# Chunks of 64 keys for the decay product of a state-space mixer: quarters of the matmul array, and 20 pieces of decay table

## The chip, the cores and the metric

The kernel runs on one core of a Trainium2 chip. The time is the device time of one execution in microseconds, and the median of three runs is compared. Besides the runs there is one profiled execution with a trace of every instruction.

The engines named here are TensorE (matmuls, PE in the views; PEld is its weight load), VectorE (DVE), ScalarE (ACT), GpSimd (POOL) and SyncE (SP), which issues all DMA transfers of this kernel. Each engine takes its instructions in the order in which they stand in its queue.

## The reference

Three layers follow each other on x, four batches of 256 positions by 512 features: a causal attention with an adapter, a state-space mixer, and a clustered feed-forward layer. A feed-forward layer with the same weights also stands between attention and mixer. The change is in the mixer alone. Cut to what matters, the mixer computes for each of its 128 heads (64 features each, 8 groups of heads that share B and C):

```python
dt  = softplus(dt + dt_bias);  dA = dt * A            # (batch, position, head)
cum = cumsum(dA)                                      # in chunks; only differences are used
scores[i, j] = (C[i] . B[j]) * exp(cum[i] - cum[j]) * dt[j]     for j <= i, else 0
y[i] = sum_j scores[i, j] * x[j]  +  D * x[i]
```

The reference carries a state from chunk to chunk; written out over the 256 positions of a batch this is one masked product of keys j and queries i. B, C and x are projections of the normalised input with a short causal convolution of four taps and a SiLU; y is gated by the SiLU of another projection, normalised by group and projected back to 512 features. Everything is float32.

## The kernel before, in words

**Tiling.** The 8192 features of the mixer are 64 blocks of 128, two heads a block. The main loop (`for i in range(NB + 1)`) takes one block a step. All four batches, 1024 positions, stand side by side on the free axis, so a tile is 128 by 1024. Eight steps make a group, and for each group one block of B and one of C is projected in addition.

**Projections.** `projected` makes a 128 by 1024 tile `pp` in PSUM (two buffers). A product of full precision is three fp32r matmuls of 512 columns per 128 features of the input (`mm3`, L113 to L115), so one projection is 24 matmuls. The weights are fetched as `wr`, split into a high and a low part by `split` (L105 a cast on ACT, L106 a subtraction on DVE, in the first steps on POOL), and held in three buffers `w`.

**Convolution.** `conv` scales `pp` on ACT (L962), adds three taps on DVE (L969) and applies the SiLU on ACT in place (L973). The result of x is the tile `acc`, tag `x2`.

**Scores of a group.** `scores` (L983 to L988) multiplies B and C per batch and keeps three blocks of 128 keys by 128 queries: first keys with first queries, first keys with second queries, second keys with second queries. A triangle of ones (`tri`) zeroes what lies above the diagonal. The table `gm` has 4 x 3 x 128 = 1536 columns.

**Decay of a head.** The cumulative sum `cum` of all heads is written to DRAM (`cumd`); `rows` reads the row of a head back, repeated on all 128 partitions (`r`, 512 KB, two buffers). `differences` makes the table `em` of 1536 columns: on DVE four subtractions for the last block (L1001), on POOL one affine select that masks the first (L1005), on ACT eight exponentials of 128 columns with a bias per key (L1010, L1013) and one of 512 columns (L1011). `weighted` multiplies `em` by `gm` on DVE (L1017). Three buffers hold `em`, so a table can be begun when the product has read an older one.

**Turn and product.** `turned` transposes x on TensorE (`trx`, L1028) and multiplies it by dt on DVE (`xd`, L1029). `product` (L1043) is 16 float32 matmuls: per batch and block of 128 keys one for each of the two heads, whose 64 features are 64 columns of the array. The trace shows two records for each. `gated` adds D times x (L1053), multiplies by the gate's SiLU `gt` (L1163 makes it, L1056 uses it), sends the result to DRAM (`spill`) and sums its squares (ACT L1065, POOL L1066).

**Back projection.** For the group before, `recall` fetches pieces `gr` from DRAM, `split` makes `gh` of them, and `partial` multiplies (`pog`, 24 matmuls for 128 positions); `scaled` adds the result to `x` (L1114). Most steps hold one such part.

**Order.** The source gives the dependences and a rough order; a scheduler orders the instructions of each engine, and the queues are then fixed. Tables of ACT's functions are loaded (`ACT_TABLE_LOAD`) wherever an exponential follows a SiLU in ACT's queue or the reverse.

**Setup.** Ahead of the loop the kernel makes dt and the cumulative sum per head, transposes them (L941, L950, L954) and keeps them by key in `col_t` and `dt_t`.

## Time and profile before

| What | Value |
|---|---|
| Runs | 1879.57, 1879.75, 1885.73 us; median 1879.75 us |
| The profiled execution | 1881.0 us, span 1879.2 us, mean granted clock 0.989 |
| Attention and first feed-forward layer | about 0 to 330 us |
| Mixer's setup and first projections | about 330 to 420 us |
| Mixer's loop | about 420 to 1790 us |
| Last layer | the rest |
| Product `pyy`, L1043 | 189.1 us busy, 2048 records |
| Weighting, L1017 | 228.6 us busy, 128 instructions of 1786 ns |
| Exponentials of 128 columns, L1010 and L1013 | 165.0 and 166.5 us busy, 512 each |
| Subtractions, L1001 | 137.9 us busy, 512 |

The profiled execution's own time lies 1.25 us above the median of the runs. A group's line in the profile gives line, engine, operation, output and inputs, shape and count, then busy time in us and the mean of one in ns, and then how long its engine stood idle just ahead of it and for whom. The busy time of matmuls is a union of intervals that include the pipeline's latency, so single durations can't be summed.

### The profile page before, as it was taken

How to read it: one execution, taken by the hardware profiler on the slowest of the kernel's cores; microseconds unless marked ns; L12 is line 12 of the kernel's file. 1: busy time of each engine (PE TensorE's matmuls, PEld its weight loads, DVE VectorE, ACT ScalarE, POOL GpSimd, SP SyncE). 2: the span in 40 equal slices, each digit the busy share in tenths (PEclk: the TensorE clock that was granted, in tenths of full speed). 3: DMA queues.
4: the chain of work that ended last, by engine and by line, in shares of the span. 5: the costliest groups of instructions: out<-in, count | busy, mean ns of one | idle time of the engine just before them, and what ended most of it. 6: DMA issues, size and time to landing. Idle time of an engine off the chain costs nothing.

```text
span 1879.2 us, 29896 instructions
## 1 busy us (share of the span) xinstructions
PE 1812.6 (96%) x10706; PEld 1450.4 (77%) x10706; DVE 1464.7 (78%) x2317; ACT 1367.7 (73%) x2809; POOL 397.0 (21%) x380
## 2 busy tenths in 40 slices
PE   7999988899999999999999999999999999999997
PEld 6777767677778787887787787878887888787787
DVE  5566667789997779778977787778778877877777
ACT  6666675378897778777876786778777876877754
POOL 6332230012321111221221121112221211121200
PEclk9999999899999999999999999999999999999999
DMA  4000000135555545544545455544444545455341
GB/s 144 1 1 1 22 15 13 37 99 170 185 182 166 156 148 173 152 157 146 185 140 172 144 173 155 165 147 162 157 157 140 179 145 164 152 159 161 113 125 50
DMA packets 152772, 240.35 MB, mean 128 GB/s; under 512 B 12464, under 2 KB 77616, under 8 KB 152624
## 3 DMA queue, kind: packets, MB, share of 16 engines
q1 hardware_dynamic: 152624, 238.44, 39.8%
q8 instruction: 84, 1.38, 0.3%
q14 instruction: 64, 0.52, 0.1%
HBM read 202.75 MB, written 35.65 MB: 127 GB/s over the span
## 4 chain that ended last, share of the span: by engine, by line
PE 79%; DVE 9%; ACT 7%; issue 2%; DMA 2%; POOL 1%; SPq 0%; DVEq 0%; ACTq 0%; POOLq 0%
PE pp L113 12%; PE pp L114 12%; PE pp L115 12%; PE pyy L1043 9%; PE pog L113 6%; PE pog L115 6%; PE pog L114 6%; PE trx L1028 3%; ACT e L475 2%; DVE acc L969 2%; PE ptr L491 1%; DMA wor<-in_wout_dram 1%; PE pq L113 1%; PE pq L114 1%; PE pq L115 1%
## 5 line engine op out<-in xcount | busy, mean ns | idle before, releaser
L113 PE MATMUL pp<-mx,w 128*128 128x512 f32 (+1 forms) x1160 | 465.2, 401 | 7.9 <-DVE acc L969 7.4
L114 PE MATMUL pp<-mx,w 128*128 128x512 f32 (+1 forms) x1160 | 454.0, 391 | 0.0
L115 PE MATMUL pp<-mx,w 128*128 128x512 f32 (+1 forms) x1160 | 453.7, 391 | 0.0
L969 DVE SCALAR_TENSOR_TENSOR acc<-pp,cw_s,acc 128x1012 f32<-128x1012 f32 (+2 forms) x240 | 305.3, 1272 | 23.0 <-ACT acc L962 22.3
L1017 DVE TENSOR_TENSOR em<-em,gm 128x1536 f32<-128x1536 f32 x128 | 228.6, 1786 | 94.3 <-ACT em L1011 85.9
L113 PEld LDWEIGHTS pp<-mx,w 128*128 128x128 f32 x1160 | 218.4, 188 | 65.7 <-issue 10.2
L1005 POOL TENSOR_SCALAR_AFFINE_SELECT r<-r 128x512 f32<-128x512 f32 x128 | 148.6, 1161 | 521.9 <-DMA r<-cumd 394.8
L1066 POOL TENSOR_TENSOR sq<-sq,acc 128x1024 f32<-128x1024 f32 x55 | 132.6, 2410 | 582.1 <-ACT acc L1065 582.1
L115 PEld LDWEIGHTS pp<-mx,w 128*128 128x128 f32 x1160 | 218.4, 188 | 45.5 <-issue 0.4
L114 PEld LDWEIGHTS pp<-mx,w 128*128 128x128 f32 x1160 | 218.6, 188 | 40.6 <-issue 0.7
L105 ACT CAST w<-wr 128x512 fp32r<-128x512 f32 x144 | 88.5, 615 | 188.9 <-PE pp L114 150.2
L113 PE MATMUL pog<-wo,gh 128*128 128x512 f32 x512 | 204.7, 400 | 0.0
L115 PE MATMUL pog<-wo,gh 128*128 128x512 f32 x512 | 200.0, 391 | 0.0
L1010 ACT ACTIVATE em<-r,col_t 128x128 f32<-128x128 f32 x512 | 165.0, 391 | 48.1 <-PE pyy L1043 46.5
L114 PE MATMUL pog<-wo,gh 128*128 128x512 f32 x512 | 200.0, 391 | 0.0
L1043 PE MATMUL pyy<-em,xd 128*64 128x256 f32 (+1 forms) x2048 | 189.1, 329 | 2.4 <-DVE em L1017 2.4
L1043 PEld LDWEIGHTS pyy<-em,xd 128*64 128x64 f32 x2048 | 133.9, 137 | 63.8 <-issue 21.8
L1013 ACT ACTIVATE em<-r,col_t 128x128 f32<-128x128 f32 x512 | 166.5, 388 | 0.0
L1001 DVE TENSOR_SCALAR em<-r,col_t 128x128 f32<-128x128 f32 x512 | 137.9, 332 | 12.1 <-PE pyy L1043 10.1
L1029 DVE TENSOR_TENSOR xd<-trx,dt_t 128x512 f32<-128x512 f32 x128 | 86.3, 684 | 54.1 <-PE trx L1028 53.9
L106 DVE TENSOR_TENSOR w<-wr,w 128x512 fp32r<-128x512 f32 x139 | 97.6, 703 | 35.9 <-ACT w L105 35.4
L475 ACT ACTIVATE e<-sc,nmx 128x256 f32<-128x256 f32 (+1 forms) x256 | 104.0, 441 | 21.0 <-DVE nmx L469 20.9
(290 smaller groups left out, 3187.2 us busy)
## 6 DMA issues: line engine op xcount, KB each, us to landing
wr<-in_win_dram SPq DMA_DIRECT2D x287, 256.0 KB, 2.8
r<-cumd SPq DMA_DIRECT2D x128, 512.0 KB, 4.1
spill<-gb SPq DMA_DIRECT2D x63, 512.0 KB, 2.8
gr<-spill SPq DMA_DIRECT2D x120, 256.0 KB, 3.5
wor<-in_wout_dram SPq DMA_DIRECT2D x64, 256.0 KB, 3.1
out_dram<-x SPq DMA_DIRECT2D x8, 256.0 KB, 2.3
x<-in_x_dram SPq DMA_DIRECT2D x1, 1536.0 KB, 8.7
gr<-spill SPq DMA_DIRECT2D x8, 192.0 KB, 2.5
```

The lines of the kernel that those rows point to most:

```text
L113: nc.tensor.matmul(o, lh, rh, start=(first and k == 0), stop=False)
L114: nc.tensor.matmul(o, lh, rl, start=False, stop=False)
L115: nc.tensor.matmul(o, ll, rh, start=False, stop=(last and k == n - 1))
L475: nc.scalar.activation(es_[c][:, 2 * j + pr, :], sc[:, j, :], AF.Exp, bias=nm[:, j : j + 1], accum_out=rs[:, c, h : h + 1],)
L969: nc.vector.scalar_tensor_tensor(av[:, :, d:], pv[:, :, : L - d], cw_s[:, ch, tap : tap + 1], av[:, :, d:], ALU.mult, ALU.add,)
L1001: nc.vector.tensor_scalar(e[:, b, 2, :], rv[:, b, 1, :], col_t[:, h, b, 1:2], 0.0, ALU.subtract, ALU.min,)
L1005: nc.gpsimd.affine_select(rv[:, :, 0, :], rv[:, :, 0, :], pattern=[[0, B], [1, P]], compare_op=ALU.is_ge, fill=-1e30, base=0, channel_mult ...
L1010: nc.scalar.activation(e[:, b, 1, :], rv[:, b, 1, :], AF.Exp, bias=col_t[:, h, b, 2:3])
L1013: nc.scalar.activation(e[:, b, 0, :], rv[:, b, 0, :], AF.Exp, bias=col_t[:, h, b, 0:1])
L1017: nc.vector.tensor_tensor(e, e, gm, ALU.mult)
L1043: nc.tensor.matmul(py[d, b, k * P :], xd[:, 2 * b + k, d], es2[hh][:, b, 2 * k : 2 if k == 0 else 3, :].rearrange("p s i -> p (s i)"), sta ...
L1066: (nc.gpsimd if n < NB - 1 else nc.vector).tensor_tensor(sq, sq, x2, ALU.add)
```

## The change

The keys of a batch are now cut into four chunks of 64. Two batches share the 128 partitions: partitions 0 to 63 hold chunks of batch j, partitions 64 to 127 the same chunks of batch 2 + j (u is the half, j is 0 or 1). Per j and chunk c only the queries from the chunk on are kept: 4, 3, 2 and 1 pieces of 64, so ten for each j and 20 pieces of 64 in all, 1280 columns.

- `product` takes 64 keys and 64 features at a time: 32 matmuls of 256, 192, 128 or 64 columns, for two partition halves and two heads, each on its own quarter of the array. The two halves write two PSUM banks.
- `scores` makes `gm` in 20 pieces, without a triangle: 16 matmuls, each half of the keys on its own column half, and eight copies on DVE.
- `differences` makes the 20 pieces: pieces of a chunk with itself (`own`, 512 columns) by one subtraction on DVE, one addition of a mask (`past`) on POOL and one exponential; pieces of the next chunk, where a pair of chunks begins (`next_`, 256 columns), by one subtraction and one exponential; the others by four exponentials of 128 columns, with a bias `end_t`.
- `rows` reads two halves of a row, each repeated on 64 partitions, with four buffers of half the size.
- `conv` of x now keeps `acc` apart (one buffer) and writes the SiLU to `x2` in the new order of positions; `gated` works in two halves of 512.
- The setup writes dt and the cumulative sum in the new order as well; the sum restarts at the same places as before.

```diff
             def scores(bt, ct):
-                gm = p2.tile([P, B, 3, P], F32, name="gm", tag="gm")
...
+                gm = p2.tile([P, 20, Q], F32, name="gm", tag="gm")
+                for j in range(2):
+                    for cs in ((0, 1), (2, 3)):
+                        pg = ps.tile([P, 512], F32, name="pg", tag="m")
...
+                                nc.tensor.matmul(
+                                    pg[u * Q : (u + 1) * Q, at : at + n], bt[:, o : o + Q],
+                                    ct[:, o : o + n], start=True, stop=True,
+                                )
...
             def rows(h):
-                r = p2.tile([P, NT], F32, name="r", tag="r", bufs=2)
-                load(r, cumd[h : h + 1, :].to_broadcast([P, NT]))
+                r = p2.tile([P, 2 * L], F32, name="r", tag="r", bufs=4)
+                for u in range(2):
+                    load(
+                        r[u * Q : (u + 1) * Q, :],
+                        cumd[h : h + 1, u * 2 * L : (u + 1) * 2 * L].to_broadcast([Q, 2 * L]),
+                    )
                 return r
             def differences(h, r):
-                e = p2.tile([P, B, 3, P], F32, name="em", tag="em", bufs=3)
...
+                e = p2.tile([P, 20, Q], F32, name="em", tag="em", bufs=3)
+                own, next_ = pieces_of(e, 0, 4, 4, 7), pieces_of(e, 1, 8, 2, 9)
+                rv = r.rearrange("p (j c i) -> p j c i", j=2, c=4)
+                cv = col_t[:, h, :].rearrange("p (j c) -> p j c", j=2).unsqueeze(3)
+                nc.vector.tensor_tensor(own, rv, cv.to_broadcast([P, 2, 4, Q]), ALU.subtract)
+                nc.gpsimd.tensor_tensor(
+                    own, own, past.unsqueeze(1).unsqueeze(1).to_broadcast([P, 2, 4, Q]), ALU.add
+                )
+                nc.vector.tensor_tensor(
+                    next_, rv[:, :, 1::2, :], cv[:, :, 0::2].to_broadcast([P, 2, 2, Q]), ALU.subtract
+                )
+                for j in range(2):
+                    for c in range(2):
+                        nc.scalar.activation(
+                            piece(e, j, c, 2 - c, 2), rv[:, j, 2:, :], AF.Exp,
+                            bias=end_t[:, h, 2 * j + c : 2 * j + c + 1],
+                        )
+                nc.scalar.activation(next_, next_, AF.Exp)
+                nc.scalar.activation(own, own, AF.Exp)
                 return e
             def product(xd, es2):
-                py = ps_y.tile([P, B, L], F32, name="pyy", tag="pyy")
...
+                py = ps_y.tile([P, 2, 2 * L], F32, name="pyy", tag="pyy")
+                for j in range(2):
+                    for c in range(4):
+                        for u in range(2):
+                            us = slice(u * Q, (u + 1) * Q)
+                            for hh in range(2):
+                                d = slice(hh * PD, (hh + 1) * PD)
+                                nc.tensor.matmul(
+                                    py[d, u, j * L + c * Q : (j + 1) * L].rearrange("p (k i) -> p k i", i=Q),
+                                    xd[us, 4 * j + c, d], piece(es2[hh], j, c)[us],
+                                    start=(c == 0), stop=(c == 3),
+                                )
                 return py
             def gated(n, x2, gt, py, sq):
-                nc.vector.scalar_tensor_tensor(
-                    gb, x2, dh[:, n : n + 1], py.rearrange("p b t -> p (b t)"), ALU.mult, ALU.add
-                )
+                for u, h in enumerate(hs):
+                    k = lambda v: v.rearrange("p (k i) -> p k i", i=Q)
+                    nc.vector.scalar_tensor_tensor(
+                        k(gb[:, h]), pair(x2)[:, :, u], dh[:, n : n + 1], k(py[:, u]), ALU.mult, ALU.add
+                    )
...
-            rr = {h: rows(h) for h in range(2)}
+            rr = {h: rows(h) for h in range(4)}
```

In `conv` of x:

```diff
-                silus.append(nc.scalar.activation(acc, acc, AF.Silu).ins)
-                return acc
+                x2 = p2.tile([P, NT], F32, name="x2", tag="x2", bufs=2)
+                silus.append(nc.scalar.activation(
+                    pair(x2).rearrange("p k u i -> p u k i"),
+                    acc.rearrange("p (u k i) -> p u k i", u=2, i=Q), AF.Silu,
+                ).ins)
+                return x2
```

The new helpers `piece` and `pieces_of` only address pieces of a table: `piece(v, j, c, k, n)` gives n query pieces of chunk c from the k-th on, with a step of 1 or 3 pieces, and `pieces_of` gives every n-th piece for both j at once.

## The prediction

> **What bounds the kernel now.** I read the page's first part, then its chain, then a table by stretches, because 96% busy is an average and matmuls overlap in it. The stretches are four consecutive steps of the mixer's loop over its 64 head pairs, cut where the decay product `pyy` starts.
>
> ```profile
> PE 1812.6 (96%) x10706; PEld 1450.4 (77%) x10706; DVE 1464.7 (78%) x2317; ACT 1367.7 (73%) x2809; POOL 397.0 (21%) x380
> PE 79%; DVE 9%; ACT 7%; issue 2%; DMA 2%; POOL 1%; SPq 0%; DVEq 0%; ACTq 0%; POOLq 0%
> ```
> ```profile
> 950.54:970.83 20.29, 20.29 (x113) 16.22 (x112) 15.98 (x22) 14.82 (x29) 5.73 (x4) 1.00 0.46 143
> 970.83:991.13 20.30, 20.30 (x113) 16.23 (x112) 15.90 (x23) 14.82 (x29) 3.72 (x3) 1.00 0.48 155
> 991.13:1011.42 20.29, 20.29 (x113) 16.22 (x112) 15.55 (x22) 14.81 (x29) 3.77 (x4) 1.00 0.49 155
> ```
>
> The columns are stretch, length, then busy PE, weight loads, DVE, ACT, POOL, then clock and DMA. A regular step is 20.29 us and TensorE has no hole in it; DVE works 15.9, ACT 14.8. Eight such steps make a group, some with fewer or more matmuls. So the mixer (420 to 1790 us) is bound by TensorE, and DVE and ACT have 4.4 and 5.5 us to spare per step. Where that spare time lies is seen in the timeline of ACT: it stands 3.95 us until a projection gives back a weight buffer, and 1.25 us until the product is over.
>
> ```profile
> 1011.31 0.62 ACT L105 CAST w<-wr 128x512 fp32r<-128x512 f32 x1 [3.95 <-PE pp L114]
> 1014.28 1.28 ACT L1010 ACTIVATE em<-r,col_t 128x128 f32<-128x128 f32 x4 [1.25 <-PE pyy L1043]
> 1018.51 1.28 ACT L973 ACT_TABLE_LOAD   x1
> 1019.81 1.06 ACT L973 ACTIVATE acc<-acc 128x1024 f32<-128x1024 f32 x1
> ```
>
> How fast the product runs comes from TensorE's timeline, at a place where its first matmul stands alone (two records[...]) and at one where it is whole:
>
> ```profile
> 922.15 0.65 PE L1043 MATMUL pyy<-em,xd 128*64 128x256 f32 x2
> 922.73 0.50 PE L113 MATMUL pp<-mx,w 128*128 128x512 f32 x1
> ...
> 1011.43 2.82 PE L1043 MATMUL pyy<-em,xd 128*64 128x256 f32 x32
> 1014.18 0.50 PE L113 MATMUL pp<-mx,w 128*128 128x512 f32 x1
> ```
>
> The lone matmul streams 2 x 256 = 512 columns and the next work starts 0.58 us later. The whole product streams, for each head, 4 batches x (256 + 128) x 2 = 3072 columns, and takes 2.75 us. If the two heads, which lie on two column halves of the array, run side by side: (2.75 - 0.58) / (3072 - 512) = 0.85 ns a column and 0.15 us for entering and leaving. One after the other they would need over 5 us, so they do run side by side.
>
> [...] No run here shows quarters of 64 by 64; the nearest row is attention's `sc` (64 rows, two row halves, fp32r), whose eight matmuls take 0.61 us to the next operation, 1536 columns that at the projections' 0.23 us per 512 would need 0.69 us in turn and some edge more. [...] The trace has 1283 ns[...] (load at 1018.51, SiLU at 1019.81), so I use 1.28. [...] The `py` products of attention, 16 matmuls, are over 0.79 us after their start (200.64 to 201.43 us), 50 ns each at most[...]; a burst of 64 no run shows.
>
> **The change part by part.**
>
> *Product.* Per key chunk the queries kept are 256, 192, 128 and 64. A quarter streams 2 batches x 640 x 2 = 2560 columns: 2560 x 0.85 = 2.17, with the edge 2.32 us against 2.75. Gain 0.43 us per step, all on the binding engine: 64 x 0.43 = 27.5 us. It issues 64 matmuls for 32. [...] I take the stream.
>
> *Order of the product.* In the built programs the first product matmul stands alone, parted by projections, at 13 steps; in the trace of before at 11. Two more at 0.58 us: +1.2. In later groups the new `pg` matmuls stand inside a product; some 0.3 us of edges, against 0.43 us that `pg` saves by the same columns: nothing.
>
> *Elementwise work, DVE.* Weighting falls from 1536 to 1280 elements: 128 x (1.67 x 256/1536 = 0.28) = -36 us. Differences: 512 instructions, 138 us, give way to 256 of 512 and of 256 elements, by the rows of 512 at 0.60 and half of it: 128 x 0.93 = 119, -19. Gating in two halves +8. `gm` copies about as before. DVE some 47 us less.
>
> *ACT.* Per head 8 exponentials of 128 (2.59 us) become 4 (1.30) and one of 256, between 0.29 and 0.63, say 0.37; the one of 512 stays. That is -0.92 x 128 = -118 us. But in the built order ACT changes its table 297 times, before 195: a regular step has four loads, not two, since exponentials now stand on both sides of the SiLU of x and of the gate's SiLU. 102 x 1.283 = +131 us. Net +13 us of 1368.
>
> *POOL* trades an affine select (1.16 us) for an add of 512 (`r`, L301: 1.29), which now stands between DVE's difference and ACT's exponential; its own square sum, 2.4 us, is queued there too. By the order both adds are done 5 us before ACT comes to them. *SP* issues two row loads for one, 128 more, with half the bytes (512 to 256 KB a head) and four buffers for two: hidden, rows come two heads earlier. *Setup*: two more ACT copies of 512, +1.
>
> *What is late next.* ACT, DVE and TensorE now hang together in one ring per step, because the queues are in order. Following the built order: three taps 3.90; load 1.28; SiLU of x 1.06; load 1.28; one exponential 0.29; square 1.04; load 1.28; gate SiLU 1.00; load 1.28; exponentials 0.37 and 0.63: 13.4. Then DVE: weighting 1.39, `x` 0.66, `xd` 0.60, two splits 1.20, weighting 1.39, two splits 1.20: 6.4, and the next taps. With 0.15 for handovers this is 20.0 us, and TensorE needs 20.29 - 0.43 = 19.86. So a regular step ends at about 20.0, not 19.86: what waits is the transposition `trx` behind the SiLU. Bounds of the ring: 19.6 if the exponentials of 256 and the weightings come out shorter, 20.7 if [...]a `gh` cast waits for its transfer (it does for up to 4 us nine times before). Some 30 steps are regular: 30 x 0.14 = +4.2. Steps with extra projections have room.
>
> *Sum* against the profiled execution (1881.0 us with a span of 1879.2, 1.25 over the median 1879.75): -27.5 + 1.2 + 4.2 + 1 = -21, so 1860 there, 1859 as a median.
>
> **Rivals.**
>
> *The ring swallows it.* The spare time of ACT goes into table loads, the ring comes to 20.3 to 20.6, and `trx` waits. For it: four loads in a ring that I can close only to a few tenths. Against: none of its durations is a guess by more than 0.1. Regular steps then cost 0 to 0.3 more than before, other steps gain 0.43: 30 x 0.15 - 34 x 0.43 + 2 = -8 in the middle, so 1866 to 1886.
>
> *The quarters do not run four at a time* (ends slower). If the two row halves take turns, a product has 5120 columns: 4.35 + 0.15 = 4.50 us, 64 x 1.75 = +112, some 1990 us. [...] It decides from a product above 2.75 us. For it: no run of float32 on row halves. Against: column halves in float32 and row halves in fp32r overlap[...].
>
> *More comes back than the product.* Fewer DVE passes and earlier rows also end the 9 us in which projections wait behind ACT and DVE: 1842 to 1850.
>
> **How the numbers follow.** First case 0.58, time 1859, own range 1848 to 1869; the ring 0.18; the quarters 0.14; more 0.10. About 0.5% (9.4 us) is what a measurement here can tell from no change. Faster: most of the first case and all of the last, 0.62. Same: part of the ring and the edge of the first, 0.17. Slower: the quarters and the ring's end, 0.21. The range takes the first, the last and the ring, 1842 to 1900, and leaves out the quarters.
>
> **What would show it.** The product: 64 records in about 2.35 us, four starting together; 2.75 or more refutes the main step. Table loads: 297. A regular step between 19.8 and 20.1 us with a small wait of `trx` for the SiLU of x; 20.3 or more with ACT's wait for `pp` gone is the ring. ACT busy near 1380, DVE near 1420.

## The result, and the profile after

The changed kernel takes 1934.76 us (median of four runs, 1932.12 to 1938.86) against 1882.12 us of the kernel before on the same chip: ratio 1.028, 95% interval 1.0251 to 1.0309. It is slower by 2.8%, where the prediction had 1859 us and a range up to 1900. The profiled execution is 1932.1 us with a span of 1930.3.

From the page of the changed kernel, the engines' busy time and the shares of the chain that ended last:

```profile
PE 1816.3 (94%) x12882; PEld 1455.3 (75%) x12882; DVE 1493.3 (77%) x2157; ACT 1396.1 (72%) x2527; POOL 482.0 (25%) x380
PE 46%; DVE 21%; ACT 20%; issue 5%; DMA 4%; POOL 3%; SPq 0%; ACTq 0%; DVEq 0%; POOLq 0%
```

TensorE's part of the chain fell from 79% to 46%: it now waits for others. The product itself does what was forecast. In TensorE's timeline of the changed kernel (start, length, operation, shape, count) a whole product is 64 records, and the next work starts 2.34 us after the product's start (the rounded times of these lines give 2.35), where the kernel before needed 2.75. So the product is 0.41 us shorter:

```profile
1016.92 0.39 PE L115 MATMUL pp<-mx,w 128*128 128x512 f32 x1
1017.23 2.41 PE L1089 MATMUL pyy<-em,xd 64*64 64x256 f32 x64
1019.58 0.50 PE L113 MATMUL pp<-mx,w 128*128 128x512 f32 x1
```

The table by stretches of the changed kernel (stretch, length, busy PE, weight loads, DVE, ACT, POOL, clock, DMA) shows two regular steps, and the step at the end of a group, in which C is projected and the next group's scores are made:

```profile
997.12:1017.23 20.11, 20.05 (x145) 16.13 (x144) 16.31 (x20) 15.79 (x25) 5.79 (x3) 1.00 0.43 131
1017.23:1037.34 20.11, 20.04 (x145) 16.14 (x144) 16.30 (x20) 15.79 (x25) 5.80 (x3) 1.00 0.43 130
...
923.33:949.48 26.15, 21.70 (x157) 16.16 (x156) 22.74 (x30) 17.85 (x27) 5.86 (x3) 0.87 0.42 131
```

A regular step is 20.11 us, as forecast (20.0) and 0.18 less than before. The step at the group's end is cut where the main part of each product starts, since in both kernels the first two records of the second product run ahead. It is 26.15 us; in the kernel before the same step is 19.82 us (stretch 903.80 to 923.62). The seven steps of this kind take 23.1 to 26.7 us, before 18.8 to 20.8. Measured from the end of one product to the end of the next, the span's 51 us split as follows:

| Stretch | before, us | after, us | difference |
|---|---|---|---|
| to the end of the first product | 427.4 | 431.5 | +4.1 |
| first group (nothing yet to project back) | 118.2 | 127.6 | +9.4 |
| groups 2 to 7, each | 179.8 to 180.9 | 185.6 to 187.3 | +35.3 in all |
| last group | 166.3 | 168.7 | +2.4 |
| after the last product | 85.1 | 85.0 | -0.1 |

So there are two questions: why the ends of groups lost 6 us each, and why the product's 0.41 us shows as only 0.2 in regular steps.

Where TensorE's time went is seen when the loop is cut from the end of the first product to the end of the last (stretch, length, busy PE first, then the columns of the table above), in the kernel before and in the changed one:

```profile
427.69:1794.40 1366.71, 1353.63 (x7415) 1080.00 (x7415) 1113.12 (x1514) 1057.04 (x1892) 277.06 (x180) 1.00 0.50 159
```

```profile
431.71:1845.57 1413.86, 1355.77 (x9539) 1083.71 (x9539) 1141.27 (x1352) 1085.90 (x1619) 362.34 (x182) 0.99 0.41 130
```

Length less busy time is what TensorE stands idle: 13.1 us before, 58.1 after. Its busy time has not fallen, although 64 products at 0.41 us less are worth 26 us; part of the reason is a lower clock (0.99 against 1.00 in these lines), as is shown below.

**The end of a group.** The timeline of the changed kernel there (a bracket holds the wait before the instruction and what ended it):

```profile
923.33 2.07 PE L1089 MATMUL pyy<-em,xd 64*64 64x256 f32 x46
...
928.12 2.40 PE L1013 MATMUL pg<-bc 128*64 128x256 f32 x16 [2.71 <-ACT bc L993]
...
930.45 1.54 PE L1089 MATMUL pyy<-em,xd 64*64 64x192 f32 x18
...
933.50 1.70 PE L1013 MATMUL pg<-bc 128*64 128x256 f32 x16
...
934.91 1.02 DVE L1021 COPY gm<-pg 128x256 f32<-128x256 f32 x4 [3.26 <-PE pg L1013]
...
936.51 1.40 DVE L1101 SCALAR_TENSOR_TENSOR gb<-x,dh,pyy 128x512 f32<-128x512 f32 x2
...
937.82 0.68 DVE L1043 TENSOR_TENSOR em<-r,col_t 128x512 f32<-128x512 f32 x1
...
938.65 2.13 POOL L1044 TENSOR_TENSOR em<-em,past 128x512 f32<-128x512 f32 x1 [25.41 <-DVE em L1043]
...
940.82 0.63 ACT L1057 ACTIVATE em<-em 128x512 f32<-128x512 f32 x1 [5.54 <-POOL em L1044]
```

The scores' matmuls `pg` stand in the middle of the product, and TensorE waits there 2.71 us for C's SiLU while the product's last 18 records stand behind. DVE has the copy of the second score tile ahead of everything else and idles 3.26 us for it; the gate `gb` and the subtraction L1043 come after that. POOL's mask add can only follow the subtraction, and ACT stands 5.54 us for POOL, with the square, the gate's SiLU and the other exponentials behind it. The next product is then late: its main part starts at 949.48 us. One wait runs through four queues. Over the loop TensorE waits 17.9 us in seven times for C's SiLU at `pg`, and 12.4 us in seven times for the weighted table ahead of a product.

**A wait can be paid twice.** In stretches after such waits of the same kernel the clock column falls to 0.50 to 0.60:

```profile
928.12:931.20 3.08, 3.08 (x31) 2.42 (x32) 3.04 (x7) 1.91 (x3) 0.00 (x0) 0.50 0.52 180
931.92:934.90 2.98, 2.98 (x16) 1.85 (x17) 0.00 (x0) 2.97 (x9) 0.00 (x0) 0.60 0.17 61
1135.62:1139.63 4.01, 4.00 (x62) 3.72 (x63) 4.01 (x5) 1.91 (x3) 0.00 (x0) 0.57 0.71 215
```

The last of them is a product (62 records) that took 4.0 us instead of 2.3. Between 440 and 1800 us the changed kernel has 16 gaps of TensorE over 1.5 us between starts, 39 us in all; the kernel before has none. Eight of the sixteen were followed by half clock, seven times for 3.4 us and once for 6.8, 31 us together. By an estimate from these lengths, half of their time, that is worth at most 15 us of the 51. In the kernel before the clock doesn't fall in this stretch (1.00). The eight gaps have 2.1 to 3.7 us between starts, but their length alone does not decide: after a gap of 2.13 us at 947 us the next product took 2.3 us, after one of the same length at 1133 us it took 4.0.

### The profile page after: what moved, and what is told of

Read it like the earlier page. It is cut to its first block, busy times and chain, and to the rows that moved or that the text cites. A ratio compares the mean times of both kernels' runs of the same rounds, so it can differ in the third digit from the quotient of the medians.

```text
span 1930.3 us, 33621 instructions
## 1 busy us (share of the span) xinstructions
PE 1816.3 (94%) x12882; PEld 1455.3 (75%) x12882; DVE 1493.3 (77%) x2157; ACT 1396.1 (72%) x2527; POOL 482.0 (25%) x380
## 4 chain that ended last, share of the span: by engine, by line
PE 46%; DVE 21%; ACT 20%; issue 5%; DMA 4%; POOL 3%; SPq 0%; ACTq 0%; DVEq 0%; POOLq 0%
DVE acc L988 8%; PE pp L113 5%; PE pp L114 5%; PE pp L115 5%; PE pog L113 5%; PE pog L115 5%; PE pog L114 4%; ACT L996 2%; ACT x L996 2%; PE trx L1072 2%; PE pyy L1089 2%; ACT e L475 2%; DMA r<-cumd 2%; DVE em L1061 2%; POOL em L1044 2%
## 5 line engine op out<-in xcount | busy, mean ns | idle before, releaser
L1044 POOL TENSOR_TENSOR em<-em,past 128x512 f32<-128x512 f32 x128 | 229.9, 1800 | 1045.7 <-DVE em L1043 992.3
L1061 DVE TENSOR_TENSOR em<-em,gm 128x1280 f32<-128x1280 f32 x128 | 195.8, 1530 | 169.3 <-ACT em L1057 139.6
L988 DVE SCALAR_TENSOR_TENSOR acc<-pp,cw_s,acc 128x1012 f32<-128x1012 f32 (+2 forms) x192 | 244.3, 1272 | 23.3 <-ACT acc L981 20.4
L1052 ACT ACTIVATE em<-r,end_t 128x128 f32<-128x128 f32 x512 | 169.2, 392 | 45.9 <-PE pyy L1089 45.2
L1089 PE MATMUL pyy<-em,xd 64*64 64x192 f32 (+3 forms) x4096 | 176.6, 310 | 13.9 <-DVE em L1061 13.9
L1089 PEld LDWEIGHTS pyy<-em,xd 64*64 64x64 f32 x4096 | 142.9, 138 | 58.5 <-issue 24.1
L1114 POOL TENSOR_TENSOR sq<-sq,x 128x1024 f32<-128x1024 f32 x55 | 137.6, 2501 | 25.2 <-ACT x L1113 25.2
L113 PEld LDWEIGHTS pog<-wo,gh 128*128 128x128 f32 x512 | 96.1, 188 | 24.7 <-ACT rg L1140 2.0
L115 PEld LDWEIGHTS pog<-wo,gh 128*128 128x128 f32 x512 | 96.1, 188 | 20.8 <-DVE gh L106 0.3
L106 DVE TENSOR_TENSOR gh<-gr,gh 128x512 fp32r<-128x512 f32 (+1 forms) x128 | 86.0, 678 | 33.2 <-ACT gh L105 33.2
```

The source lines that it names most:

```text
L113: nc.tensor.matmul(o, lh, rh, start=(first and k == 0), stop=False)
L115: nc.tensor.matmul(o, ll, rh, start=False, stop=(last and k == n - 1))
L988: nc.vector.scalar_tensor_tensor(av[:, :, d:], pv[:, :, : L - d], cw_s[:, ch, tap : tap + 1], av[:, :, d:], ALU.mult, ALU.add,)
L1044: nc.gpsimd.tensor_tensor(own, own, past.unsqueeze(1).unsqueeze(1).to_broadcast([P, 2, 4, Q]), ALU.add)
L1052: nc.scalar.activation(piece(e, j, c, 2 - c, 2), rv[:, j, 2:, :], AF.Exp, bias=end_t[:, h, 2 * j + c : 2 * j + c + 1],)
L1061: nc.vector.tensor_tensor(e, e, gm, ALU.mult)
```

## The experiments

All times are medians, and each ratio is against the kernel before on the same chip. Not all runs were on one chip; the kernel before took 1881 to 1885 us on them, so times that differ by less than some 4 us are not told apart. The three runs with the old product leave out the right pairing of keys: they multiply the new tables in the old pattern and give other values. Gains below are in us between medians; sums by group come from the profiled execution of each run.

| Run | us | ratio to before, 95% interval |
|---|---|---|
| changed kernel | 1934.76 | 1.028 (1.0251 to 1.0309) |
| mask add on DVE | 1914.38 | 1.0168 (1.015 to 1.0186) |
| scores later | 1916.01 | 1.0178 (1.0161 to 1.0195) |
| both | 1904.06 | 1.0099 (1.008 to 1.0118) |
| mask on POOL first | 1907.40 | 1.0116 (1.0092 to 1.014) |
| mask on POOL first, scores later | 1901.54 | 1.0101 (1.0087 to 1.0116) |
| kernel before with a POOL add | 1901.31 | 1.0085 (1.0067 to 1.0103) |
| exponentials together | 1936.55 | 1.0283 (1.0264 to 1.0301) |
| the three | 1916.21 | 1.0164 (1.0144 to 1.0184) |
| exponentials together in the first group | 1904.87 | 1.0114 (1.0096 to 1.0132) |
| exponentials together, pool first, scores later | 1922.11 | 1.0211 (1.0193 to 1.0229) |
| exponentials together, pool first, scores later, SiLU primed | 1917.27 | 1.0182 (1.0158 to 1.0206) |
| changed kernel, old product | 1912.96 | 1.0158 (1.014 to 1.0175) |
| pool first, scores later, old product | 1892.61 | 1.0051 (1.0038 to 1.0065) |
| transposes later | 2035.48 | 1.0813 (1.0788 to 1.0838) |
| pool first, scores later, transposes later | 2021.94 | 1.0743 (1.0724 to 1.0763) |
| pool first, scores later, transposes later, old product | 1893.38 | 1.006 (1.0047 to 1.0073) |
| pool first, scores later, transposes later, exponentials together | 2001.89 | 1.0638 (1.0616 to 1.066) |
| setup's taps later, squares on DVE | 1898.83 | 1.0073 (1.0057 to 1.009) |

### The chain through the mask and the scores

**Mask add on DVE.**

```diff
-                nc.gpsimd.tensor_tensor(
+                nc.vector.tensor_tensor(
                     own, own, past.unsqueeze(1).unsqueeze(1).to_broadcast([P, 2, 4, Q]), ALU.add
```

> The changed kernel with the mask's addition of L1044 on DVE instead of POOL, nothing else. Theory P (the add on POOL stands between DVE's subtraction and ACT's exponential in queues that run in order, and ACT waits 5.5 us for it in the step where a group of eight ends): those steps fall from 26.1 to about 21 us, 7 of them 35 us, so about 1900 us, while the regular step stays at 20.1. Theory G (the scores' matmuls inside the product are what holds that step: PE waits there for C's SiLU, and all else is late after that): the step keeps at least 24 us, and the kernel is at 1920 to 1935. Theory T (ACT's extra table loads set the pace): 291 loads instead of 297, so no more than 5 us, 1930.

Groups 3 to 7 fall from 185.6 to 187.3 us to 182.2 to 185.4, the regular step stays at 20.1, the first two groups together stay where they were (314 us). The gain is 20 us of the 35 that theory P claimed. The steps that it named fall only to 22.2 to 25.2 us and not to 21; the step after each of them is 1 to 2 us shorter in six of seven cases. So P has a part of the cause and not the whole. TensorE still waits for C's SiLU at `pg` (14.5 us in seven times).

**Scores later.**

```diff
-                        gms[g + 1] = scores(bt, ct)
+                        late = (g + 1, bt, ct)
...
                     sqs[m // GB] = gated(m, px2, gt, py, sq)
+                if late:
+                    gms[late[0]] = scores(*late[1:])
+                    late = None
```

> The changed kernel with the scores of the next group written after the product and its gate instead of before them, nothing else. G: PE's wait for C's SiLU inside the product (2.7 to 3.3 us, seven times) goes, and with it DVE's wait for the second scores tile (3.3 us): the step where a group ends falls from 26.1 us to 20 or 21, so about 1895 to 1900 us. P: the add on POOL still follows DVE's subtraction late, so the step stays at 24 us or over and the kernel above 1920. T: 307 loads instead of 297, so no gain, 1935 to 1945.

19 us, and groups 3 to 7 at 182.8 to 183.9. Theory G was right on the place: the step where a group ends falls to 20.0 to 22.2 us. It was wrong on the reason and on the sum, since the step after it grows in six of seven cases, by 0.3 to 3.9 us. TensorE's wait for C's SiLU does not go (16.2 us, against 17.9 in the changed kernel). What goes is its place inside the product. In the timeline of this run the product is whole before the wait, and gate, subtraction and POOL's add come 3.8 to 5.9 us earlier than in the lines shown above:

```profile
922.79 2.41 PE L1089 MATMUL pyy<-em,xd 64*64 64x256 f32 x64
...
927.44 1.52 PE L1013 MATMUL pg<-bc 128*64 128x256 f32 x16 [2.24 <-ACT bc L993]
...
930.61 1.40 DVE L1101 SCALAR_TENSOR_TENSOR gb<-x,dh,pyy 128x512 f32<-128x512 f32 x2
...
933.99 0.68 DVE L1043 TENSOR_TENSOR em<-r,col_t 128x512 f32<-128x512 f32 x1
...
934.82 1.33 POOL L1044 TENSOR_TENSOR em<-em,past 128x512 f32<-128x512 f32 x1 [22.14 <-DVE em L1043]
```

**Both** edits above.

> The changed kernel with both: scores written after the product's gate, mask's addition on DVE. Alone each gave about 20 us (1914 and 1916). If the wait of PE for C's SiLU inside the product (P's and G's chains one after the other) are two separate waits, the gains add: 1896. If both take away the same slack, it stays at 1910 to 1914. The first group is not touched by either (17.3 us a step) and the regular step stays at 20.1.

31 us of the 39 that the two gave singly: mostly two costs, in part the same slack.

**Mask on POOL first.** Same operations and engines, in the other order.

```diff
-                nc.vector.tensor_tensor(own, rv, cv.to_broadcast([P, 2, 4, Q]), ALU.subtract)
                 nc.gpsimd.tensor_tensor(
-                    own, own, past.unsqueeze(1).unsqueeze(1).to_broadcast([P, 2, 4, Q]), ALU.add
+                    own, rv, past.unsqueeze(1).unsqueeze(1).to_broadcast([P, 2, 4, Q]), ALU.add
                 )
+                nc.vector.tensor_tensor(own, own, cv.to_broadcast([P, 2, 4, Q]), ALU.subtract)
```

> The changed kernel with the two operations that make the diagonal pieces swapped: POOL adds the mask to the row of sums first, straight after its load, and DVE subtracts the column afterwards. Same number of instructions, sizes and engines. If the gain of putting the add on DVE came from the order (DVE, then POOL, then ACT in queues that run in order), this gives as much or nearly: 1914 to 1918, with ACT's waits for POOL gone. If it came from POOL's own speed, or from DVE and POOL holding each other up while both run on two operands, no gain: 1930 to 1937.

27 us, more than the order was thought to be worth. ACT's waits for POOL at this exponential are gone (40.4 us in the changed kernel). The groups in this run show a second effect:

```profile
L1043 POOL TENSOR_TENSOR em<-r,past 128x512 f32<-128x512 f32 x128 | 174.1, 1382 | 769.3 <-PE pyy L1089 511.5 <-ACT acc L981 145.1 <-DMA wr<-in_win_dram 84.1
...
L1047 DVE TENSOR_TENSOR em<-r,col_t 128x256 f32<-128x256 f32 x128 | 54.7, 428 | 0.0
```

In the changed kernel the add has a mean of 1800 ns and the subtraction of 256 elements, which DVE takes up while POOL adds, 820 ns. Here they have 1382 and 428. So the order both keeps ACT from waiting for POOL and shortens the add and the subtraction. What each of the two is worth was not separated.

**Mask on POOL first, with scores later.**

> The changed kernel with the mask added on POOL before DVE's subtraction (1907 alone) and the scores written after the gate (1916 alone). The first takes the chain through POOL out of the end of each group (its second step 16.8 us) but leaves PE's wait for C's SiLU inside the product (31 us for the step before it, seven times); the second takes that to 27.3. If the two are separate costs: 1907 - 7 x 3.7 = about 1881. If the slack is shared as with the add on DVE (1904 for the pair): 1898 to 1904. First group unchanged at 17.3 to 17.7 us a step.

6 us less than the mask alone, with intervals that overlap: the slack is shared here. Groups 3 to 7 are at 180.2 to 181.1 us, as in the kernel before (179.8 to 180.6). With that the ends of groups are repaired, and what is left over the kernel before lies ahead of the end of the first product (8.1 us, of which the changed kernel has 4.1), in the first group (+7.8) and in the second (+2.1). The same cut of the loop as above gives:

```profile
435.70:1814.68 1378.98, 1339.77 (x9539) 1075.39 (x9539) 1080.89 (x1350) 1095.60 (x1627) 300.78 (x181) 1.00 0.42 133
```

TensorE stands idle for 39.2 us here, 26 us more than in the kernel before: as much as the shorter products save. It waits 14.8 us for DVE's taps ahead of projections, 12.7 us for C's SiLU at `pg` and 5.6 us for x at the transposes. By an estimate from the clock column (1.00 stands for 0.995 or more, over 1379 us) half clock is worth 7 us at most here, against at most 15 in the changed kernel, so up to 15 of the 33 us gained may be the clock.

**The kernel before with a POOL add.**

```diff
                         ALU.subtract, ALU.min,
                     )
+                nc.gpsimd.tensor_tensor(
+                    e[:, :, 2, :], e[:, :, 2, :],
+                    tri[:, P : 2 * P].unsqueeze(1).to_broadcast([P, B, P]), ALU.mult,
+                )
```

> The kernel before, with one operation added in the same place: after DVE's subtractions for the third block a POOL tensor_tensor of 512 elements (a multiplication by ones, so no value changes) that ACT's exponential of it then waits for. Orders of PE and the 195 table loads stay as they are. If the step through POOL is enough by itself to cost what the changed kernel lost at group ends: plus 15 to 35 us, 1900 to 1920. If POOL's and DVE's contention is what it costs: DVE's busy time rises by 30 us or more. If it needs the late scores ahead of it, the kernel before hides it: 1882 to 1888.

+17 us (23 in the profiled execution, in which this is split). It is not the order at group ends: groups 3 to 7 rise by 0.5 to 1.4 us each, and 11 us fall in the first group. DVE's busy time rises by 115 us although DVE got no work. The groups of this run:

```profile
L1021 DVE TENSOR_TENSOR em<-em,gm 128x1536 f32<-128x1536 f32 x128 | 251.7, 1966 | 94.0 <-ACT em L1015 86.0 <-ACT em L1017 8.0
...
L1005 POOL TENSOR_TENSOR em<-em,tri 128x512 f32<-128x512 f32 x128 | 216.9, 1694 | 445.4 <-PE pp L115 294.3 <-DVE em L1001 133.7 <-ACT acc L1069 17.3
...
L1001 DVE TENSOR_SCALAR em<-r,col_t 128x128 f32<-128x128 f32 x512 | 201.6, 452 | 12.0 <-PE pyy L1047 11.3 <-DMA r<-cumd 0.7
```

The weighting goes from 1786 to 1966 ns and the subtractions from 332 to 452. A POOL step is thus not enough by itself to stop a group's end; in the changed kernel the late subtraction stands ahead of it. But it has a price of its own, paid on DVE.

### Table loads

**Exponentials together.**

```diff
-                    nc.scalar.activation(gt, pp, AF.Silu)
+                    gate = nc.scalar.activation(gt, pp, AF.Silu).ins
...
-                        with tc.issue_after(silus[2]) if i == 0 else ExitStack():
+                        with tc.issue_after(gate):
```

> The changed kernel with the exponentials of a step held behind its gate's SiLU on ACT, nothing else: 167 table loads instead of 297, 130 x 1.28 = 167 us of ACT's busy time less. T: the steps of the first group return from 17.3 to about 15 us (16 us in all), the regular steps from 20.1 to 19.9 (some 40 of them, 8 us), and the end of each group gains the two loads that stand ahead of the weighting (2.6 us, seven times): about 1893 us. G or P: the end of each group stays within 1 us of 26.1, and only the first group gains, so 1910 to 1920. If the loads cost nothing because ACT had room: 1935.

ACT's busy time falls by 180 us to 1215.9 and the time by nothing. The first group gains 3 us (16.8 a step), regular steps 0.1. The second group (6 us more) and what lies outside the groups (6 us more) take it back. The block of twelve exponentials now stands ahead of C's SiLU in ACT's queue, and TensorE's wait at `pg` rises from 17.9 to 32.8 us in seven times, up to 7.1. So the extra table loads are not worth 42 us, as theory T had it. What they cost at the ends of groups is not shown, since the same edit makes TensorE wait longer there.

**The three:** exponentials together, add on DVE, scores later.

> The changed kernel with all three: add on DVE, scores after the gate, exponentials behind the gate's SiLU (167 table loads). In the run with the exponentials together DVE was at 32.4 of 33.6 us in two steps of the first group because its subtraction (0.68 us) took 1.76 us beside POOL's adds. If table loads and POOL's adds together hold the first group, its steps fall from 17.3 to 15.1 to 15.5 (-12 us) and the regular steps to 20.0 or under; with the boundary as in the run of the two alone (1896 expected there) that is 1880 to 1888, about the time of the kernel before. If holding the exponentials back makes the weighting late at the end of a group (36 us for that step when it was done alone), these steps eat the gain: 1900 to 1915.

The second case of the expectation, at its edge: first group 127.2, later groups 180.6 to 184.8, and 12 us slower than without holding the exponentials.

**In the first group only,** with mask on POOL first and scores later: `issue_after(gate)` where `i < GB`.

> As the run before it, with the exponentials held behind the gate's SiLU in the first eight steps only (two table loads a step there instead of four). If the four loads in ACT's ring are what holds the first group at 17.3 us a step, and POOL's adds no longer stand beside DVE's subtractions, five steps fall to 15.1 to 15.6: 9 to 12 us less than the run before it. If DVE (slowed beside POOL) is the next bound there, as with the exponentials together alone (16.8): 2 to 3 us less.

"The run before it" is the one with mask on POOL first and scores later. The result lies within that run's interval. The first group takes 124.7 us instead of 126.0, with steps mostly of 16.7, so the loads were worth some 0.2 us a step there. The timeline of this run holds the clearest view of DVE beside POOL:

```profile
471.66 1.29 DVE L1073 TENSOR_TENSOR xd<-trx,dt_t 128x512 f32<-128x512 f32 x2
...
472.54 2.40 POOL L1114 TENSOR_TENSOR sq<-sq,x 128x1024 f32<-128x1024 f32 x1 [3.08 <-ACT x L1113]
...
472.87 2.62 DVE L1046 TENSOR_TENSOR em<-em,col_t 128x512 f32<-128x512 f32 x1
...
475.41 0.41 DVE L1047 TENSOR_TENSOR em<-r,col_t 128x256 f32<-128x256 f32 x1
```

The subtraction, 0.68 us elsewhere, began 0.33 us after POOL's add and ended 0.55 us after it: it got hardly anywhere until POOL was done. Two of DVE's operations that have one of their two inputs in PSUM did not take longer beside POOL: the two `xd` above took 1.29 us together although the second ran beside the add. In the trace of the changed kernel from 427 to 1800 us `xd` has a mean of 681 ns both in the 73 cases beside a POOL operation and in the 48 others, and in that of the kernel before a tap L969 has 1272 ns both in 22 cases beside one and in 207 others.

### The product's own worth

**Changed kernel with the old product.**

```diff
+                for b in range(B):
+                    for k in range(2):
+                        for hh in range(2):
+                            d = slice(hh * PD, (hh + 1) * PD)
+                            at = (0, 4, 10, 14)[b] + 2 * k
+                            nc.tensor.matmul(
+                                py[d, b // 2, (b % 2) * L + k * P : (b % 2 + 1) * L],
+                                xd[:, 2 * b + k, d],
+                                es2[hh][:, at : at + 4 - 2 * k, :].rearrange("p k i -> p (k i)"),
+                                start=(k == 0), stop=(k == 1),
+                            )
```

> The changed kernel with the product alone put back to the form of the kernel before: sixteen matmuls of 128 keys instead of sixty-four of 64, on the same tables (the values are then not those of the reference: pieces of the two batches are added together). If the product's own gain is real and nothing else hangs on it: 0.43 us more in each of 64 products, 27 us, so 1962 us. If the planner's order hangs on the number of the product's matmuls (with sixteen it puts the scores behind the product again and ACT has 218 table loads instead of 297): the end of each group falls from 26.1 to about 20 us (-42) and the first group's steps to 15.5 (-14), so 1935 + 27 - 56 = 1906 us.

22 us faster, with a product that is 0.41 us slower. (Counted as instructions the two products have 16 and 32 matmuls; the "sixty-four" of the expectation are the new one's records.) It is the expectation's second case: the scheduler's order is another one when the product has sixteen matmuls. It puts `pg` behind the product again (that step, from product end to product end, 27.5 us instead of 31.6 to 33.8).

**Mask on POOL first, scores later, old product.**

> As the first run of this call (mask on POOL first, scores after the gate), with the product alone in the form of the kernel before: sixteen matmuls of 128 keys (the values are then not the reference's). Where PE sets the pace the product's 0.42 us comes back, in 64 products less the five or six of the first group where it doesn't: regular steps 20.3 instead of 20.05, in all plus 15 to 25 us. If the product's gain isn't worth anything in time: within 5 us.

Neither case: 9 us faster than with the new product, the intervals apart. Regular steps rise from 20.05 to 20.3, but the first group falls from 126.0 to 122.0 and the steps after a group's end by 1 to 2 us. The cut of the loop shows what is traded:

```profile
435.71:1806.93 1371.22, 1358.04 (x7530) 1078.79 (x7529) 1091.45 (x1353) 1059.06 (x1598) 322.59 (x181) 1.00 0.42 134
```

TensorE works 18 us more than with the new product and idles 26 us less (13.2 against 39.2). The waits that go are those at `pg` for C's SiLU (12.7 us, here none among the matmuls' waits), and about 5 us each of those for DVE's taps and for x at the transposes. The order of TensorE differs too. Counted from the start of a product in a regular step, the transposes start 9.2 us later with the old product (9.7 in the kernel before). With the new one it is 8.1 us, straight behind the gate's 24 matmuls. The product is 0.41 us shorter, and in the order made for it the four matmuls of the next projection that stood between are gone. The way over ACT and DVE to x has not become shorter. No run has the new product in the order of the old one, so what the order alone costs stays open.

### The transposes

The next runs test theory W: regular steps lose the rest of the product's gain because TensorE waits at the transposes for x, the SiLU's result. In the changed kernel it waits up to 0.5 us there in each of the four regular steps from 997 to 1077 us.

**Transposes later,** on the changed kernel: the first four transposes of a step are written after the output's matmuls.

```diff
                     xd = next(turning)
-                    next(turning)
                 for _ in range(PER.get(gi, 0)):
...
                 if i < NB:
+                    next(turning)
                     for _ in turning:
```

> The changed kernel with the first four transposes of a step written after the output's matmuls instead of before them, nothing else. Theory W: the regular steps fall from 20.1 to 19.87, the sum of PE's own work (35 of them, 8 us), and the step after each group's end by 0.5 to 1 us; the scores' wait and the add on POOL stay: 1915 to 1927. If the transposes' wait only moves to the next thing that needs x (the product's em or the conv's buffers): 1932 to 1937.

**The same on the repaired kernel** (mask on POOL first, scores later).

> Mask on POOL first, scores after the gate (1901.5 together), and the transposes behind the output's matmuls. W: regular steps 19.87 instead of 20.05, the second step of each group 27 instead of 28.3 to 29: 35 x 0.2 + 7 x 1.5 = 17 us less, about 1885. If ACT's ring with its four table loads is the real bound of the regular step, it stays at 20.05 and the kernel above 1898.

100 and 120 us slower, regular steps at 22 to 24 us: a new wait, not a test of the old one. The timeline of the second:

```profile
1019.76 1.49 DVE L1061 TENSOR_TENSOR em<-em,gm 128x1280 f32<-128x1280 f32 x1 [5.39 <-ACT em L1057]
...
1021.17 0.74 DVE L1162 SCALAR_TENSOR_TENSOR x<-pog,rg,x 128x512 f32<-128x512 f32 x1
...
1021.97 0.66 PE L1072 MATMUL trx<-con,x 128*128 128x128 f32 x4 [1.85 <-DVE x L1162]
```

The transposes need the PSUM tile that DVE's L1162 gives back, and L1162 stands in DVE's queue behind a weighting that waits 5.39 us for ACT.

**The same with the old product,** and **with the new one and the exponentials together:**

> The run before it with the product alone in the form of the kernel before (values not the reference's). W: nothing of PE waits in the regular steps of either, so the product's own price shows: 20.28 against 19.87 in some 35 to 42 regular steps and as much in the others that PE sets, 15 to 24 us more than the run before it, about 1903. If the shorter product still isn't worth anything, as in the pair before: 1880 to 1890.

> As e13 with the exponentials of all steps held behind the gate's SiLU (167 table loads instead of 307, 180 us less of ACT's time). If table loads cost no time any more once PE's order has the slack: within 4 us of e13. If ACT's ring still holds steps of the first group and the second of each group: 8 to 15 us less. If holding the exponentials back makes the weighting late at the end of groups (36 us a step when done alone): 5 to 20 us more.

("e13" is the run on the repaired kernel.) The old product's order hardly minds the edit (1893.4), and 194 us less of ACT's work bring only 20 us back. None of the four reads the product's price.

**SiLU primed.** Here TensorE's order stays nearly as it is and x comes early. Both runs hold the exponentials together (mask on POOL first, scores later); the second adds:

```diff
+                with tc.issue_after(first_):
+                    nc.scalar.activation(stat.tile([P, 1], F32, name="prime"), ones[:, 0:1], AF.Silu)
```

where `first_` is the convolution's first operation on ACT.

> Mask on POOL first, scores after the gate, exponentials of all steps held behind the gate's SiLU (167 table loads). Regular steps 20.0 as in the run with the exponentials together, transposes waiting 0.2 us each step. By the runs of the parts: first group 16.8, end of groups 27.4 and 19 to 25, so 1895 to 1910.

> The same with SiLU's table loaded ahead: a one-element SiLU after the convolution's first operation, in each step. The table load leaves the path from DVE's last tap to x, which comes 1.28 us earlier. Theory W: the transposes no longer wait, regular steps fall from 20.0 to 19.87 or less; in all 35 x 0.15 = 5 us, and more where the steps after a group's end hang on x: 5 to 15 us less than the control. If the regular step is held by something else, it stays at 20.0 and the kernel within 3 us of the control.

The control, at 1922 us, missed its own forecast of 1895 to 1910: as in the run of the three, holding all exponentials back costs more than the loads it saves.

The waits of the transposes for x, from the control and then from the primed kernel (total, times, longest):

```profile
PEld trx L1072 <- ACT x L996: 20.1, 43, 0.9
...
PE trx L1072 <- ACT x L996: 4.0, 7, 0.6
```

```profile
PEld trx L1074 <- ACT x L998: 4.5, 8, 0.6
...
PE trx L1074 <- ACT x L998: 1.2, 7, 0.2
```

Regular steps fall from 20.0 to 19.86 us, which is TensorE's own work as it was forecast, 20.29 less 0.43. Theory W holds for regular steps. In the whole time the 5 us between the two lie within the intervals, since other steps moved both ways: in the primed run TensorE waits 23.8 us in six times for DVE's copies of the scores, in the control 0.6 us once.

### Setup and first group

**Setup's taps later, squares on DVE** in the first eight steps, on the run with the first group's exponentials together.

```diff
+                    with tc.issue_after(scan) if inner and ch == 0 else ExitStack():
...
-                    (nc.gpsimd if n < NB - 1 else nc.vector).tensor_tensor(sq, sq, x2, ALU.add)
+                    (nc.gpsimd if GB <= n < NB - 1 else nc.vector).tensor_tensor(sq, sq, x2, ALU.add)
```

> The run with the first group's exponentials held together (mask on POOL first, scores after the gate; 1904.9), with two more edits. In the setup DVE's taps of the first x block are held behind the second half's scan: with batches on the partition halves no transpose of the sums can start before both scans, and the taps stood between them. If that is the setup's loss, the first product ends 3 to 4 us earlier (433.2 before); if not, within 1 us. In the first eight steps the sum of squares is added on DVE instead of POOL: there DVE's subtraction of 0.68 us took 2.62 us while POOL added. If DVE and POOL holding each other up is what keeps these steps at 16.7 us, they fall to 15.3 to 16; if DVE's own work sets them, they stay or rise to 17.5. In all 1893 to 1900 in the first case of both.

The second scan and the first transpose of the sums come 1.3 us earlier than in the run without the two edits, and the first product ends 1.1 us earlier. So the product follows the scan, but the edit moved the scan too little to show whether this is the whole loss. The first group stays at 16.7 us a step although the subtraction is back at 0.68 us, so the squares' add beside DVE is not what holds it. This is the fastest version that has the new product, still 0.73% slower than the kernel before; no run is faster than the kernel before.

## Why the prediction was wrong, step by step

**Product, right in size, wrong in worth.** 0.43 us was forecast, 0.41 measured. The quarters run four at a time, their records starting 6 to 7 ns apart, so that rival falls: in turns the product would have needed 4.50 us by the estimate, and it took 2.34. That the starts of its 64 records would not limit it was the author's estimate; in the product at 1017 us they lie within 2.19 us. The step that failed is "64 x 0.43 = 27.5 us", all on the binding engine. It takes for granted that TensorE stays without holes. Instead its idle time in the loop went from 13.1 to 58.1 us. A regular step gained 0.2 us (29 such steps in groups 2 to 8, 6 us). The rest of a regular step's gain went to the transposes' wait for x. That is shown by the primed pair, with the exponentials held together, where 19.86 us is reached once x comes earlier. In the other 35 steps the gain went into waits at the ends of groups and in the first group. Even with the ends repaired TensorE idles 26 us more than before, which is all that the products save.

**"Inside-product `pg` matmuls: nothing."** The second failed step. I counted columns and edges and not what `pg` waits for, nor what stands behind it: the product's rest, then DVE's gate and subtraction. Moving the scores was worth 19 us. In the built order the place could be seen. The wait for C's SiLU was there before too, 0.64 us at 908 us, but behind the whole product.

**"By the order both adds are done 5 us before ACT comes to them."** The third. In a regular step it holds: in the one from 997 to 1017 us the adds are done 4.9 and 5.6 us ahead. At the end of a group, which I did not check, ACT waited 5.5 us. Putting the add on DVE was worth 20 us, doing it first 27.

**POOL's add at 1.29 us, the subtraction of 256 at 0.33.** Mis-sized: 1.80 and 0.82, since each stands in the other's way; the prediction put that at nothing. Apart from POOL's add the subtraction takes 0.42 us. DVE came out at 1493 us busy instead of about 1420. In the run with the add on DVE, with the add's own 97.7 us taken off, DVE is at 1417. So POOL's add cost DVE 76 us, 51 of them in this subtraction. ACT was 1396 for 1380, with the 297 loads as forecast.

**The ring** of 20.0 us: right for regular steps (20.1). I took the first group as TensorE's own. It is a ring as well there, as the chain of waits through one step of the changed kernel shows (start, length, what; ACT L1211 and ACT L1056 without a tile are table loads):

```profile
479.88 1.26 DVE acc L988
...
484.25 1.27 DVE acc L988
485.52 1.31 DVE gb L1101 x2
486.83 0.61 DVE em L1043
...
487.58 2.49 POOL em L1044
...
490.09 0.63 ACT em L1057
490.73 0.95 ACT x L1113
...
491.69 1.12 ACT L1211
...
492.99 1.02 ACT gt L1211
...
494.03 1.28 ACT L1056
...
495.77 1.13 DVE em L1061
...
497.18 1.26 DVE acc L988
```

No TensorE in it, and the same tap comes again after 17.3 us (479.88 and 497.18 us) where the kernel before took about 15. POOL's add and two table loads lie in the chain. The runs that took either away, or both, still had steps of some 16.7 to 17.7 us in the mean. What closes the ring then stays open.

**Setup** was taken as +1 and is +4.1. With two batches on the partition halves a transpose of the sums needs both scans; the first starts at 413.8 us instead of 404.8. That 4 of these 9 us reach the first product is read from the traces. The one attempt on it brought the second scan 1.3 us earlier and the product 1.1. That fits, but it tests only a part of the 4 us.

## What to carry to other kernels

A gain on the binding engine is worth its size only as long as nothing that this engine waits for becomes the later one: write down for each wait of that engine how early its data is now, and subtract the gain from that. Where a scheduler orders the queues, check the steps that differ from the regular one (here the ends of groups) with the new dependences, instruction by instruction: a new hand-over between in-order queues costs what is queued behind it (here DVE stood 3.26 us and ACT 5.54 us in one step). An operation put on GpSimd was not free for VectorE (115 us of busy time in the kernel before with a POOL add): count the VectorE operations that it can hold up. In these traces there were among them two-operand operations with both inputs in SBUF (0.68 to 2.62 us in the case shown), and the subtractions L1001, which read one tile and a column (332 to 452 ns in the mean).

## What had not been expected of the hardware

- 32 float32 matmuls of 64 by 64 in four quarters (64 records, with as many weight loads) take 2.34 us. An estimate fits that: 2560 columns in each quarter at 0.85 ns, the rate worked out for 128 by 64, and 0.17 us for entering and leaving.
- Eight of sixteen gaps of 1.5 to 3.7 us between TensorE's starts were followed by half clock, for 3.4 or 6.8 us: a product took 4.0 instead of 2.3 us, `pp` matmuls started 426 ns apart instead of 227.
- A DVE subtraction of 0.68 us took 2.62 us beside one POOL add; one more POOL operation per head cost DVE 115 us of busy time in the kernel before.
